# Moving one-operand steps to ScalarE and sharing tile buffers across a layer seam in a four-layer graph kernel

## The chip, the cores and the metric

The kernel runs on one core of one Trainium2 chip. The metric is the device time of one execution in microseconds (us). Engines are named as in the profile: PE is TensorE (PEld its weight loads), DVE is VectorE, ACT is ScalarE, POOL is GpSimd, SP is SyncE, which issues the large loads.

## What is computed

Four graph layers act on `x` (4096 x 64) with one dense 4096 x 4096 matrix `adj`. Each layer normalises `x`, applies relu, and adds its result to `x`. Cut to what matters:

```
h = relu(layernorm(x))
layer 0:  x += relu((adj @ h) @ W0.T + b0)
layer 1:  h', q, k = three "lorentz" linear maps of h
          a = adj * sigmoid(att(q, k));  s = a @ h';  x += s / sqrt(|inner(s, s)|)
layer 2:  log_ij = logmap(h_i, h_j) on the Poincare ball, weights adj / rowsum(adj)
          x += expmap(0, (sum_j w_ij log_ij) @ W2 + b2)
layer 3:  mask = adj != 0;  rank = cumsum(mask) along a row
          weight 0.5 ** (last 100 neighbours, counted from the end);  x += (w @ h) @ W3 + b3
```

All of it is float32, with bfloat16 where values are exact (masks, ranks, split terms).

## The kernel before, in words

**Tiles.** `adj` is read transposed, in groups of 128 partitions x 2 x 512 float32 (512 KB). A block `ib` is 512 columns of the output (8 blocks); a group `g` is 256 rows of the sum (16 groups). A unit of work is one (block, group).

**Layer 0** (`l0_sums`): four matmuls per unit into `acc`; VectorE adds the groups up into `dg` for the degrees. Groups 3, 7, 11, 15 (`LEFT`) of blocks 0 to 6 are added in layer 1 instead (`group`, line 801). At the end of a block `after0` and `before1` turn the rows into layer 1's `HL`, `qT`, `kT`.

**Layer 1**, in pairs of units: `l1_atts` (products `mm<-qT,kT`), `l1_sigmoids` (ScalarE, out of `mm`), `l1_weights` (VectorE, times `adj`), `l1_sums` (`acc<-sig,HL`). Products use two PSUM tiles `mm`, so a product waits until the sigmoid before last has read its tile. There are `SIG` = 6 tiles `sig`. At a block's end `after1` (line 566) copies `acc` to `e`, multiplies by `twice`, copies the result to `h`, squares it, and updates `x`; `before2` (line 450) then makes layer 2's operands `RT`, `LT`, `RB`, `LB`, `HA` and columns `Mc`, `Qc`, `Fc` out of the block's rows. This chain is called the row chain here; nearly all of it is VectorE work on 128 x 256 tiles or on columns of four.

**Layer 2** runs over `work`: 72 items (`ib` <= `J`, two halves). For one item: `l2_dists` (`mm<-RT,LT`, `mm<-RB,LB`), `l2_squares` (ACT Square, `v<-mm`), `l2_clamps` (DVE on `v`), `l2_signs` (PE, adds to the same `mm`), `l2_roots` (ACT Ln, Exp, Exp: `v<-v`, `t<-v`, `v<-v`), `l2_coshs` (DVE `t<-mm,t`), `l2_logs` (ACT `t<-t`), `l2_pairs` (DVE `t<-t,v`), `l2_weights` (DVE `w<-t,adj`), `l2_sums` (PE `acc<-w,HA`). An item with `ib` < `J` is also used turned: `l2_turns` (PE), `l2_weights2` (DVE), `l2_sums2` (PE). Ln and Exp need another table of ScalarE than the sigmoid; `log_exp_tables` loads it. Item 14 is the first that uses the rows of block 7.

The seam: `second_part` (line 956) closes layer 1's pools when the last sum is planned, opens the pool `w2` in the same memory, loads the table and lets VectorE fill `fars`. `v` and `t` (three tiles each) lie in `w2`; `l2_squares` (line 997) therefore asks for `opened["second"]`.

**Layer 3**: `l3_masks` (DVE, `adj` != 0 into the memory of `RT`, `LT`, `RB`, `LB`), `l3_counts` (PE `pick`, DVE copy `total`, PE `spread`, DVE copy `chunks`; twice a block), `l3_ranks` (line 1268: per pair four products with `near`, four with `fars` and `chunks`), `l3_weights` (ACT, two reads of `mm` per pair), `l3_sum` (eight products with `S3`). `l3_ranks` puts one or two sums after each pair of ranks, if their operands are planned.

**Order.** Each engine runs its instructions in a fixed order, which the kernel's own planner makes at build time: `Pace` (line 58) holds when each engine and tile is expected to be free, by rough costs; one load is costed at 1.45 us (line 116). `in_turn` (line 702) takes, of the threads' next steps and of the row chains in `tail`, the one that can start first; a row chain wins ties by `EPS`. So a step whose expected time changes moves to another place in its queue, and steps around it too.

Of the kernel before, what the change touches and what calls it, by code (L numbers as in the profile page):

```python
# [41 lines left out]
MAX_NEIGH = 100  # L42
STEP = 128.0
EPS = 0.01
TURN = "PE"
ON_V, ON_S = "DVE", "ACT"
UP = 2.0 ** (127 - MAX_NEIGH)
# [10 lines left out]
class Pace:  # L58
# [54 lines left out]
        self.latest = max(self.latest, end)  # L113

    def load(self, t):
        self.free["DMA"] = max(self.free["DMA"], self.now) + 1.45
        self.ready[self.name(t)] = self.free["DMA"] + 2.0


# [16 lines left out]
def kernel(ctx: ExitStack, tc: tile.TileContext, a: dict, out: bass.AP):  # L136
# [313 lines left out]
    def before2(ib, st):  # L450
        rb, lb = rbs[slot["now"]], lbs[slot["now"]]
        h = rt("h", [P, CB, D])
        yield from layernorm_relu(ib, h)
        sq = rt("r_sq", [P, CB, D])
        DVE.tensor_mul(sq, h, h)
        n = rt("r_n", [P, CB, 1])
        DVE.tensor_reduce(n, sq, AX.X, ALU.add)
        bc = rt("r_c", [P, CB, 1])
# [14 lines left out]
        DVE.tensor_scalar(m, m, -2.0, None, ALU.mult)  # L473
        yield ON_V
        hh = rt("r2", [P, CB, 2, D])
        for k in range(2):
            DVE.tensor_mul(hh[:, :, k, :], h, ic.to_broadcast([P, CB, D]))
        DVE.tensor_copy(HA[:, cs(ib), 0:D], hh[:, :, 0, :])
        l = rt("l2", [P, CB, D])
        DVE.tensor_scalar(l, hh[:, :, 0, :], -2.0 * SC, None, ALU.mult)  # L480
        yield from transposed(hh.rearrange("p c k d -> p c (k d)"), P, RT[:, ws(ib)])

        v, b = rt("r_v", [P, CB, 2, 1]), rt("r_b", [P, CB, 2, 3])
        DVE.tensor_copy(v[:, :, 0, :], ic)
# [80 lines left out]

    def after1(ib, acc, st):
        e = rows.tile([P, W], F32, tag="e", name="e")
        DVE.tensor_copy(e, acc)
        st["acc_free"][ib % 2] = pace.latest
        yield ON_V, lambda: st["dg_done"].get((1, ib)) if (1, ib) in st["dg"] else 0.0  # L570
        dg = st["dg"].get((1, ib))
        if dg is not None:
            DVE.tensor_add(dg[:, 0, :], dg[:, 0, :], dg[:, 1, :])
        yield TURN
        ps = bank()
        v, n = ps[:, 0 : CB * D].rearrange("p (c k) -> p c k", k=D), CB * D
        for c in range(CB):
            b = slice(c * P, (c + 1) * P)
            PE.matmul(v[:, c, :], e[:, b], twice, start=True, stop=True)
            if dg is not None:  # L580
                PE.matmul(ps[:, n + c : n + c + 1], dg[:, 0, b], ones_f, start=True, stop=True)
        if dg is not None:
            st["dg_free"][ib % 2] = pace.latest
        yield ON_V
        if dg is not None:
            DVE.tensor_add(
                deg[:, cs(ib), :], deg[:, cs(ib), :], ps[:, n : n + CB].unsqueeze(2)
            )
        s = rt("h", [P, CB, D])
        DVE.tensor_copy(s, v)  # L590
        sq = rt("r_sq", [P, CB, D])
        DVE.tensor_mul(sq, s, s)
        n = rt("r_n", [P, CB, 1])
        DVE.tensor_reduce(n, sq[:, :, 1:D], AX.X, ALU.add)
        DVE.tensor_sub(n, n, sq[:, :, 0:1])
        m = rt("r_m", [P, CB, 1])
        DVE.tensor_scalar(m, n, -1.0, None, ALU.mult)
        DVE.tensor_max(n, n, m)
        DVE.tensor_scalar(n, n, 1e-08, None, ALU.max)
        power(n, n, -0.5)  # L600
        yield ON_V
        DVE.tensor_mul(s, s, n.to_broadcast([P, CB, D]))
        DVE.tensor_add(x[:, cs(ib), :], x[:, cs(ib), :], s)
        yield ON_V
# [97 lines left out]
    def in_turn(threads):  # L702

        waiting = [[gen, next(gen, None)] for gen in threads]
        waiting = [t for t in waiting if t[1]]
        while waiting or tail:
            best = None
            for k, entry in enumerate(tail):  # L710
                if k < 2 or entry["evicts"]:
                    need = entry["need"]() if entry["need"] else 0.0
                    if need is None or (entry["on"] == TURN and not spare):
                        continue
                    start = max(entry["at"], pace.free[entry["on"]], need)
                    if best is None or start < best[0]:
                        best = start, entry
            for thread in waiting:
                on, need = thread[1]
                t = need()  # L720
                if t is not None and (best is None or max(t, pace.free[on]) < best[0] - EPS):
                    best = max(t, pace.free[on]), thread
            pace.now, what = best
            if what in tail:
                advance(what)
                continue
            pace.latest = 0.0
            what[1] = next(what[0], None)
            if what[1] is None:
                waiting.remove(what)  # L730
# [54 lines left out]
    def pair_tiles_free():  # L785

        a, b = (d.get("read") for d in pair_tiles[-2:])
        return latest(a, None if b is None else b - 0.8)

    early = ExitStack()  # L790
    p01 = early.enter_context(tc.tile_pool(name="p01", bufs=1))
    w01 = early.enter_context(tc.tile_pool(name="w01", bufs=3))
# [6 lines left out]


    def group(layer, ib, g):
        degree = (g in LEFT and ib < NB - 1) == (layer == 1)
        return {"layer": layer, "ib": ib, "g": g, "degree": degree, "left": 1 + degree, "at": 0.0}


# [94 lines left out]
    def l1_sigmoids():  # L900
        for n, d in enumerate(l1):
            yield "ACT", lambda: latest(
                d.get("dist"), l1[n - SIG].get("summed") if n >= SIG else 0.0
            )
            d["att"] = w01.tile([P, G, W], F32, tag="sig", name="sig", bufs=SIG)
# [10 lines left out]
    def l1_sums():  # L916
        for pair in pairs:
# [5 lines left out]
                d["summed"] = pace.latest  # L923
            if d["last"]:
                ib = d["ib"]
                follow(with_mark(2, ib, after1(ib, acc, st), before2(ib, st)), ON_V, evicts=True)

# [28 lines left out]
    def second_part():  # L956
# [9 lines left out]
        w2["stack"] = ExitStack()  # L966
        w2["pool"] = w2["stack"].enter_context(tc.tile_pool(name="w2", bufs=2))
        w2["others"] = w2["pool"].tile([D + 1, N], F32, name="others", bufs=1)
        log_exp_tables()
        opened["second"] = l1[-1]["summed"]  # L970
        yield "DVE", lambda: 0.0
        DVE.tensor_copy(late["fars"], far.unsqueeze(2).to_broadcast([P, NC, P]))

    def wt(name, **kw):
        return w2["pool"].tile([P, G, W], F32, tag=name, name=name, **kw)

    def l2_dists():
        for d in work:
# [73 lines left out]

    def l2_weights():
        for k, d in enumerate(work):
            yield "DVE", lambda: latest(d.get("paired"), arrival(d), ago(work, k, 2, "summed"))
            d["w"] = wt("w")
            DVE.tensor_mul(d["w"], d["t"], d["adj"])
            d["weighed"] = pace.latest
            used(d)
# [205 lines left out]
            for d in half:  # L1265
                d["chunks"] = chunks

    def l3_ranks():


        for n, pair in enumerate(pairs3):
            yield "PE", lambda: latest(
                ready(pair[0]["chunks"]) if "chunks" in pair[0] else None, pair_tiles_free(),
                work[-1].get("dist"),
            )
            chunks = []
            for d in pair:
                pair_tile(d)
                for c in range(G):
                    chunks.append((d["g"] * G + c, d["ps"][:, c, :]))  # L1280
                    PE.matmul(
                        d["ps"][:, c, :], near, d["m"][:, c, :], start=True,
                        stop=chunks[-1][0] == NC - 1, skip_group_check=True,
                    )
            for q, (c, rank) in enumerate(chunks):
                b = slice(q * Q, (q + 1) * Q)
                if c < NC - 1:
                    PE.matmul(
                        rank, late["fars"][b, c, :], pair[0]["chunks"][b, :], start=False,
                        stop=True, skip_group_check=True,  # L1290
                    )
            for d in pair:
                d["ranked"] = pace.latest
# [33 lines left out]
    def l3_sum():  # L1327
# [25 lines left out]
    last = work[L3_AT:]  # L1353
    order23 = work[:L3_AT] + [d for pair in zip(last, l3) for d in pair] + l3[len(last) :]
    in_turn([
        feed(order, "early"), feed(order23, "second"), second_part(), third_part(), l2_loads2(),
        l0_sums(), l1_sums(), l1_weights(), l1_sigmoids(), l1_atts(),
        in_steps(
            (l2_dists(), -1, once), (l2_signs(), 0, once), (l2_sums2(), 2, if_two(1)),
# [7 lines left out]
        l2_gathers(), l3_weights(), l3_ranks(), l3_counts(), l3_masks(),  # L1367
        degree_sums(0, l0), degree_sums(1, l1), constants(),
    ])

# [44 lines left out]
```

## Time and profile before

| | |
|---|---|
| time, median of 3 runs (lowest, highest) | 1216.04 us (1213.37, 1216.13) |
| profiled execution, its own time | 1215.13 us |
| span of the profiled execution | 1213.4 us |
| mean granted TensorE clock | 0.971 |
| layer 1's last sum ends | 491.15 us |
| first sum of layer 2 starts | 507.53 us |
| HBM read, written | 269.68 MB, 1.05 MB |

The times of single instructions come from the profiled execution, counted from the start of its span. A line of a timeline reads: start, duration, engine, line of the kernel, operation, output<-inputs, shapes, how many were merged, and in brackets the idle time before it with what ended it. A matmul in float32 appears as two records. All operations pass through one helper, so nearly every line says L128, and groups are told apart by their tiles. In a line of groups the numbers after the bar are busy time, mean ns of one, and idle time before with what ended it. In a line by stage the columns are start:end, length, then busy time and count of PE, PEld, DVE, ACT and POOL, the granted clock, the DMA engines' share and GB/s.

### The profile page before, as it was taken

Reading aid. Unit: us, or ns where it says so; the run is one execution under the profiler, and the core shown is the slowest. Engines: PE = TensorE matmul, PEld = TensorE weight load, DVE = VectorE, ACT = ScalarE, POOL = GpSimd, SP = SyncE. Lnnn points to the kernel's source line nnn. Section 1 sums busy time; section 2 is a strip of 40 time slices with the busy share of each in tenths; the row PEclk is TensorE's granted clock in tenths of the full one; section 3 lists DMA queues with packets and bytes.
Section 4 is the critical chain, followed back from the end, with each engine's and each line's share of the span. In section 5 each row is a group of like instructions: output and inputs, shape, how many; then the busy total and the mean of one; then the engine's idle time right before and its main releaser. Section 6 shows DMA issues by size and latency. Waiting matters only on the chain.

```text
span 1213.4 us, 15538 instructions
## 1 busy us (share of the span) xinstructions
PE 1085.3 (89%) x5368; PEld 443.9 (37%) x5368; DVE 980.9 (81%) x1621; ACT 797.6 (66%) x1204; POOL 114.7 (9%) x99
## 2 busy tenths in 40 slices
PE   4799999998999999689989979989888779999998
PEld 1244443333333333234434434444333323333333
DVE  6788789879999998779989999999989984554551
ACT  1055546666656666589898888888877775555554
POOL 2222212101101010000010010000100120000000
PEclk9899999999999999799999999989989899999999
DMA  8899999864767765335534534444444489888830
GB/s 300 326 393 373 366 362 331 328 234 141 266 227 242 250 230 181 122 120 191 178 125 160 197 105 168 145 139 156 140 156 156 144 311 361 305 306 305 300 110 9
DMA packets 77190, 271.75 MB, mean 224 GB/s; under 512 B 10040, under 2 KB 11064, under 8 KB 77112
## 3 DMA queue, kind: packets, MB, share of 16 engines
q1 hardware_dynamic: 75456, 270.57, 62.7%
q8 instruction: 42, 0.69, 0.2%
q10 hardware_dynamic: 1656, 0.20, 0.1%
q14 instruction: 36, 0.29, 0.1%
HBM read 269.68 MB, written 1.05 MB: 223 GB/s over the span
## 4 chain that ended last, share of the span: by engine, by line
PE 48%; DVE 24%; ACT 13%; issue 7%; DMA 5%; POOL 3%; ACTq 0%; SPq 0%; DVEq 0%; POOLq 0%
PE acc L128 25%; PE mm L128 15%; PE tr L128 9%; DMA adj<-in_adjT_dram 4%; DVE w L128 4%; DVE t L128 4%; ACT wt L128 4%; DVE dg L128 3%; DVE sig L128 2%; ACT v L128 2%; ACT sig L128 2%; POOL lo_s L128 2%; ACT t L128 1%; ACT lo_sq L128 1%; DVE v L128 1%
## 5 line engine op out<-in xcount | busy, mean ns | idle before, releaser
L128 PE MATMUL acc<-w,HA 128*65 128x256 f32 (+1 forms) x736 | 258.6, 488 | 20.9 <-DVE w L128 11.7
L128 ACT ACTIVATE sig<-mm,att_b,att_a 128x1024 f32<-128x1024 f32 x128 | 148.4, 1200 | 83.6 <-PE mm L128 74.8
L128 ACT ACTIVATE v<-v 128x1024 f32<-128x1024 f32 x144 | 152.1, 1057 | 47.6 <-DVE v L128 45.0
L128 ACT ACTIVATE wt<-mm 128x1024 uint16<-128x1024 f32 x124 | 120.2, 1021 | 96.1 <-PE mm L128 96.1
L128 DVE TENSOR_TENSOR sig<-sig,adj 128x1024 f32<-128x1024 f32 x128 | 151.9, 1220 | 11.1 <-ACT sig L128 10.8
L128 PE MATMUL acc<-adj,HA 128*64 128x512 f32 x512 | 127.7, 629 | 23.2 <-DVE HA L128 22.4
L128 DVE TENSOR_TENSOR dg<-dg,adj 128x1024 f32<-128x1024 f32 x113 | 137.9, 1221 | 3.4 <-DMA adj<-in_adjT_dram 2.1
L128 PE MATMUL mm<-qT,kT 64*128 64x512 f32 x512 | 131.7, 623 | 8.8 <-ACT sig L128 8.6
L128 PEld LDWEIGHTS acc<-w,HA 128*65 128x65 f32 x736 | 96.8, 142 | 112.2 <-issue 64.6
L128 PE MATMUL acc<-sig,HL 128*64 128x512 f32 x512 | 122.5, 603 | 0.8 <-DVE sig L128 0.8
L128 PE MATMUL acc<-wt,S 128*64 128x512 bf16 x496 | 99.6, 390 | 0.2 <-ACT wt L128 0.2
L128 DVE SCALAR_TENSOR_TENSOR t<-t,v 128x1024 f32<-128x1024 f32 x72 | 89.7, 1246 | 9.8 <-ACT t L128 9.8
L128 DVE SCALAR_TENSOR_TENSOR t<-mm,t 128x1024 f32<-128x1024 f32 x72 | 87.6, 1217 | 4.5 <-PE mm L128 4.2
L128 PE MATMUL mm<-RT,LT 64*128 64x512 f32 x288 | 82.6, 651 | 7.2 <-DVE t L128 7.0
L128 DVE TENSOR_TENSOR w<-t,adj 128x1024 f32<-128x1024 f32 x72 | 87.8, 1220 | 1.4
L128 ACT ACTIVATE t<-t 128x1024 f32<-128x1024 f32 x72 | 75.5, 1049 | 9.4 <-DVE t L128 9.4
L128 DVE TENSOR_TENSOR w<-tr,adj 128x512 f32<-128x512 f32 x112 | 73.2, 684 | 9.9 <-PE tr L128 9.9
L128 DVE TENSOR_SCALAR RT<-adj 128x1024 bf16<-128x1024 f32 x74 | 49.7, 690 | 37.0 <-PE mm L128 36.5
L128 ACT ACTIVATE t<-v 128x1024 f32<-128x1024 f32 x72 | 76.1, 1057 | 2.3
L128 PEld LDWEIGHTS mm<-qT,kT 64*128 64x128 f32 x512 | 42.4, 185 | 86.1 <-ACT sig L128 49.0
L128 ACT ACTIVATE v<-mm 128x1024 f32<-128x1024 f32 x72 | 72.6, 1008 | 1.6 <-PE acc L128 1.6
L128 PE MATMUL tr<-ident,t 128*128 128x128 f32 x448 | 61.0, 279 | 7.7 <-DVE t L128 4.4
(201 smaller groups left out, 1301.3 us busy)
## 6 DMA issues: line engine op xcount, KB each, us to landing
adj<-in_adjT_dram SPq DMA_DIRECT2D x512, 512.0 KB, 4.7
x<-in_x_dram SPq DMA_DIRECT2D x4, 256.0 KB, 4.1
out_dram<-h SPq DMA_DIRECT2D x8, 128.0 KB, 2.9
b<-in_b_dram ACTq DMA_DIRECT2D x2, 32.0 KB, 6.5
W<-in_W_dram ACTq DMA_DIRECT2D x3, 16.0 KB, 4.0
W0T<-in_W0T_dram ACTq DMA_DIRECT2D x2, 16.0 KB, 5.4
W1T<-in_W1T_dram ACTq DMA_DIRECT2D x1, 16.0 KB, 5.2
W1T<-in_b_dram ACTq DMA_DIRECT2D x1, 0.2 KB
```

Source lines behind the costliest of these rows:

```text
L128: done = self.tc.keep_in_program_order(getattr(self.engine, op)(*args, **kw))
```

## The change

1. Row chain: in `after1` the copies `e` and `h` and the square of the result go to ScalarE (the square reads PSUM), and the degree column is copied by ScalarE before VectorE adds it. In `before2` the square of `h`, the second half of `hh`, the copy to `HA` and the scaled copy `l` go to ScalarE; the first half of `hh` stays.
2. `sig`, `v` and `t` come from one pool `pairs` of six tiles that stays open. `v` and `t` of layer 2's first items take the places of the last `sig` tiles, each when that tile's sum is planned. The table load becomes a step of its own, `second_tables`, after the last sigmoid; `l2_weights` is now what asks for `opened["second"]`.
3. The planner costs a load at 1.37; row chains lose ties from the table load until item `FIRST` = 4 is weighed; block 0's degree is summed wholly in layer 0.
4. Layer 3: `l3_ranks` becomes `l3_pass`; where the next ranks are not ready it issues sums.

The diff, cut to its core:

```diff
+FIRST = 4
 ...
-        self.free["DMA"] = max(self.free["DMA"], self.now) + 1.45
+        self.free["DMA"] = max(self.free["DMA"], self.now) + 1.37
 ...
     def before2(ib, st):
-        DVE.tensor_mul(sq, h, h)
+        ACT.activation(sq, h, AF.Square)
+        yield ON_V
 ...
-        for k in range(2):
-            DVE.tensor_mul(hh[:, :, k, :], h, ic.to_broadcast([P, CB, D]))
-        DVE.tensor_copy(HA[:, cs(ib), 0:D], hh[:, :, 0, :])
+        DVE.tensor_mul(hh[:, :, 0, :], h, ic.to_broadcast([P, CB, D]))
+        yield ON_S
+        ACT.copy(hh[:, :, 1, :], hh[:, :, 0, :])
+        ACT.copy(HA[:, cs(ib), 0:D], hh[:, :, 0, :])
-        DVE.tensor_scalar(l, hh[:, :, 0, :], -2.0 * SC, None, ALU.mult)
+        ACT.activation(l, hh[:, :, 0, :], AF.Copy, scale=-2.0 * SC)
 ...
     def after1(ib, acc, st):
-        DVE.tensor_copy(e, acc)
+        ACT.copy(e, acc)
 ...
-            DVE.tensor_add(
-                deg[:, cs(ib), :], deg[:, cs(ib), :], ps[:, n : n + CB].unsqueeze(2)
-            )
-        DVE.tensor_copy(s, v)
-        DVE.tensor_mul(sq, s, s)
+        ACT.copy(s, v)
+        ACT.activation(sq, v, AF.Square)
+            new = rt("r_c", [P, CB, 1])
+            ACT.copy(new, ps[:, n : n + CB].unsqueeze(2))
+            DVE.tensor_add(deg[:, cs(ib), :], deg[:, cs(ib), :], new)
 ...
+                    if "tables" in opened and "weighed" not in work[FIRST]:
+                        start += 2 * EPS
 ...
+    pairp = ctx.enter_context(tc.tile_pool(name="pairs", bufs=SIG))
 ...
-        degree = (g in LEFT and ib < NB - 1) == (layer == 1)
+        degree = (g in LEFT and 0 < ib < NB - 1) == (layer == 1)
 ...
-        log_exp_tables()
+    def second_tables():
+        yield "ACT", lambda: l1[-1].get("read")
+        log_exp_tables()
+        opened["tables"] = pace.free["ACT"]
 ...
     def l2_squares():
-                opened.get("second"), d.get("dist"), ago(work, k, 3, "paired")
+                d.get("dist"), l1[2 * k - SIG].get("summed") if 2 * k < SIG else 0.0,
+                ago(work, k, SIG // 2, "paired"),
-            d["v"] = wt("v", bufs=3)
+            d["v"] = pair_buffer("v")
 ...
     def l2_roots():
-                d.get("clamped"), ago(work, k, 3, "weighed"), ago(work, k, 3, "turned")
+                d.get("clamped"), opened.get("tables"),
+                l1[2 * k + 1 - SIG].get("summed") if 2 * k < SIG else 0.0,
+                ago(work, k, SIG // 2, "weighed"), ago(work, k, SIG // 2, "turned"),
-            d["t"] = wt("t", bufs=3)
+            d["t"] = pair_buffer("t")
 ...
+    def l3_pass():
         for n, pair in enumerate(pairs3):
+            while rank_need(pair) is None:
+                yield "PE", lambda: first_of(rank_need(pair), sum_need() if sums3 else None)
+                if rank_need(pair) is None:
+                    l3_sum()
+            yield "PE", lambda: rank_need(pair)
+            l3_rank(pair)
             for _ in range(1 + n % 2):
-                t = sum_need()
-                if sums3 and t is not None:
+                if sums3 and sum_need() is not None:
                     yield "PE", sum_need
                     l3_sum()
```

More of the change, by code (lines that the diff above doesn't have):

```diff
@@ L475, in before2 @@
         hh = rt("r2", [P, CB, 2, D])
-        for k in range(2):
-            DVE.tensor_mul(hh[:, :, k, :], h, ic.to_broadcast([P, CB, D]))
-        DVE.tensor_copy(HA[:, cs(ib), 0:D], hh[:, :, 0, :])
+        DVE.tensor_mul(hh[:, :, 0, :], h, ic.to_broadcast([P, CB, D]))
+        yield ON_S
+        ACT.copy(hh[:, :, 1, :], hh[:, :, 0, :])
+        ACT.copy(HA[:, cs(ib), 0:D], hh[:, :, 0, :])
         l = rt("l2", [P, CB, D])
-        DVE.tensor_scalar(l, hh[:, :, 0, :], -2.0 * SC, None, ALU.mult)
+        ACT.activation(l, hh[:, :, 0, :], AF.Copy, scale=-2.0 * SC)
         yield from transposed(hh.rearrange("p c k d -> p c (k d)"), P, RT[:, ws(ib)])
+        yield ON_V
         v, b = rt("r_v", [P, CB, 2, 1]), rt("r_b", [P, CB, 2, 3])
@@ L583, in after1 @@
             st["dg_free"][ib % 2] = pace.latest
+        yield ON_S
+        s = rt("h", [P, CB, D])
+        ACT.copy(s, v)
+        sq = rt("r_sq", [P, CB, D])
+        ACT.activation(sq, v, AF.Square)
+        if dg is not None:
+            new = rt("r_c", [P, CB, 1])
+            ACT.copy(new, ps[:, n : n + CB].unsqueeze(2))
         yield ON_V
         if dg is not None:
-            DVE.tensor_add(
-                deg[:, cs(ib), :], deg[:, cs(ib), :], ps[:, n : n + CB].unsqueeze(2)
-            )
-        s = rt("h", [P, CB, D])
-        DVE.tensor_copy(s, v)
-        sq = rt("r_sq", [P, CB, D])
-        DVE.tensor_mul(sq, s, s)
+            DVE.tensor_add(deg[:, cs(ib), :], deg[:, cs(ib), :], new)
         n = rt("r_n", [P, CB, 1])
@@ L788, in pair_tiles_free, with pair_buffer @@
         return latest(a, None if b is None else b - 0.8)
+    pairp = ctx.enter_context(tc.tile_pool(name="pairs", bufs=SIG))
+    def pair_buffer(name):
+        return pairp.tile([P, G, W], F32, tag="pair", name=name)
     early = ExitStack()
@@ L904, in l1_sigmoids @@
             )
-            d["att"] = w01.tile([P, G, W], F32, tag="sig", name="sig", bufs=SIG)
+            d["att"] = pair_buffer("sig")
             ACT.activation(d["att"], d["ps"], AF.Sigmoid, scale=att_a, bias=att_b)
@@ L925, in l1_sums @@
                 ib = d["ib"]
-                follow(with_mark(2, ib, after1(ib, acc, st), before2(ib, st)), ON_V, evicts=True)
+                follow(with_mark(2, ib, after1(ib, acc, st), before2(ib, st)), ON_S, evicts=True)
     half = 0.25 * SC * SC
@@ L972, in second_part @@
         DVE.tensor_copy(late["fars"], far.unsqueeze(2).to_broadcast([P, NC, P]))
-    def wt(name, **kw):
-        return w2["pool"].tile([P, G, W], F32, tag=name, name=name, **kw)
+    def second_tables():
+        yield "ACT", lambda: l1[-1].get("read")
+        log_exp_tables()
+        opened["tables"] = pace.free["ACT"]
     def l2_dists():
@@ L1054, in l2_weights @@
         for k, d in enumerate(work):
-            yield "DVE", lambda: latest(d.get("paired"), arrival(d), ago(work, k, 2, "summed"))
-            d["w"] = wt("w")
+            yield "DVE", lambda: latest(
+                opened.get("second"), d.get("paired"), arrival(d), ago(work, k, 2, "summed")
+            )
+            d["w"] = w2["pool"].tile([P, G, W], F32, tag="w", name="w")
             DVE.tensor_mul(d["w"], d["t"], d["adj"])
@@ L1266, in l3_counts, with rank_need @@
                 d["chunks"] = chunks
-    def l3_ranks():
-        for n, pair in enumerate(pairs3):
[L1272 to L1293, printed above, removed]
+    def rank_need(pair):
+        return latest(
+            ready(pair[0]["chunks"]) if "chunks" in pair[0] else None, pair_tiles_free(),
+            work[-1].get("dist"),
+        )
@@ new lines, in l3_rank @@
+    def l3_rank(pair):
+        chunks = []
+        for d in pair:
+            pair_tile(d)
+            for c in range(G):
+                chunks.append((d["g"] * G + c, d["ps"][:, c, :]))
+                PE.matmul(
+                    d["ps"][:, c, :], near, d["m"][:, c, :], start=True,
+                    stop=chunks[-1][0] == NC - 1, skip_group_check=True,
+                )
+        for q, (c, rank) in enumerate(chunks):
+            b = slice(q * Q, (q + 1) * Q)
+            if c < NC - 1:
+                PE.matmul(
+                    rank, late["fars"][b, c, :], pair[0]["chunks"][b, :], start=False,
+                    stop=True, skip_group_check=True,
+                )
+        for d in pair:
+            d["ranked"] = pace.latest
@@ L1294, in l3_ranks, with first_of @@
+    def first_of(a, b):
+        return b if a is None else a
+    def l3_pass():
+        for n, pair in enumerate(pairs3):
+            while rank_need(pair) is None:
[4 more added lines that the diff above has]
+            l3_rank(pair)
             for _ in range(1 + n % 2):
-                t = sum_need()
-                if sums3 and t is not None:
+                if sums3 and sum_need() is not None:
@@ L1355 @@
     in_turn([
-        feed(order, "early"), feed(order23, "second"), second_part(), third_part(), l2_loads2(),
+        feed(order, "early"), feed(order23, "second"), second_tables(), second_part(), third_part(), l2_loads2(),
         l0_sums(), l1_sums(), l1_weights(), l1_sigmoids(), l1_atts(),
@@ L1366 @@
         ),
-        l2_gathers(), l3_weights(), l3_ranks(), l3_counts(), l3_masks(),
+        l2_gathers(), l3_weights(), l3_pass(), l3_counts(), l3_masks(),
         degree_sums(0, l0), degree_sums(1, l1), constants(),
```

## The prediction

> **What bounds the kernel now.** I read the page's shares and slices first, then busy time by stage, then each queue's timeline around the seams between layers.
>
> ```profile
> PE 1085.3 (89%) x5368; PEld 443.9 (37%) x5368; DVE 980.9 (81%) x1621; ACT 797.6 (66%) x1204; POOL 114.7 (9%) x99
> ...
> PE   4799999998999999689989979989888779999998
> ...
> PEclk9899999999999999799999999989989899999999
> ```
>
> TensorE is the bound at 89%. Its holes are the start, and the dip in the 17th slice (485 to 516 us), where the clock row also falls. Busy time by stage (columns PE, PEld, DVE, ACT, POOL, granted clock):
>
> ```profile
> 280.00:480.00 200.00, 191.01 (x856) 67.61 (x858) 185.15 (x413) 124.71 (x205) 21.01 (x12) 1.00 0.67 226
> ...
> 480.00:500.00 20.00, 13.70 (x68) 5.05 (x64) 13.46 (x21) 11.35 (x26) 1.31 (x1) 0.88 0.61 211
> 500.00:520.00 20.00, 13.39 (x42) 4.46 (x42) 16.63 (x44) 14.96 (x23) 1.01 (x1) 0.69 0.16 52
> ...
> 560.00:600.00 40.00, 40.00 (x193) 19.36 (x192) 36.74 (x42) 36.17 (x39) 0.00 (x0) 1.00 0.52 180
> ```
>
> In layer 1 TensorE is 96% and VectorE 93% busy, ScalarE 62%. In steady layer 2 TensorE has no gap. Between them 12.9 us of 40 are idle and the rest runs at a clock of 0.88 and 0.69. TensorE's timeline shows why:
>
> ```profile
> 489.21 1.94 PE L128 MATMUL acc<-sig,HL 128*64 128x512 f32 x8
> ...
> 500.70 2.08 PE L128 MATMUL mm<-RT,LT 64*128 64x512 f32 x4 [7.01 <-DVE t L128]
> ...
> 507.53 3.68 PE L128 MATMUL acc<-w,HA 128*65 128x512 f32 x4 [4.20 <-DVE w L128]
> ```
>
> Layer 1's last sum ends at 491.15, layer 2's first starts at 507.53. ScalarE and VectorE in that gap:
>
> ```profile
> 485.28 1.19 ACT L128 ACTIVATE sig<-mm,att_b,att_a 128x1024 f32<-128x1024 f32 x1
> ...
> 491.20 1.02 ACT L128 ACTIVATE v<-mm 128x1024 f32<-128x1024 f32 x1 [1.58 <-PE acc L128]
> 496.76 1.06 ACT L128 ACTIVATE v<-v 128x1024 f32<-128x1024 f32 x1 [4.54 <-DVE v L128]
> ...
> 491.81 2.28 DVE L128 COPY fars<-far 128x4096 bf16<-128x4096 bf16 x1
> ```
>
> The square of item 0 (`v<-mm`) has its input early, but its buffer lies where layer 1's tiles lay, so it waits for the last sum. Its clamp then stands behind `fars` and the last row's chain (0.69 + 2.28 + 2.9 us), so Ln starts at 496.76.
>
> Two smaller losses:
>
> ```profile
> 336.71 2.23 PE L128 MATMUL mm<-qT,kT 64*128 64x512 f32 x8 [0.45 <-ACT sig L128]
> ...
> 1123.14 0.38 PE L128 MATMUL tr<-total,spread 128*128 128x512 bf16 x1 [0.80 <-DVE total L128]
> ```
>
> In layer 1 a pair of attention products issued straight after another waits 0.45 and takes 2.23 instead of 1.92: 0.75 us. In layer 3 TensorE waits 0.80 for a total once per block of 28.29 us.
>
> **The seam between layers 1 and 2.** I count from the end of the last sigmoid, 486.47 = 0. Before: layer 2's sum of item 0 starts at 21.1, item 4 (538.28) at 51.8, item 13 at 104.4 (5.85 us an item from item 4). In the changed queues ScalarE has sigmoid, square 0, LB copy, table load, Ln, Exp; VectorE has clamp 0, `fars`, then item 0's work; layer 1's last row enters after about item 3. With the durations above: square 1.0; clamp 0.7, hidden beside LB copy 0.37 and table 1.28, to 2.7; Ln and Exp 2.1, to 4.8. `fars` moves ahead of item 0's chain and waits for the last sum (about 3.4): 5.7. So it is `fars`, not Ln, that is late next. Then cosh 1.22, log 1.05, product 1.22, weights 1.22: sum 0 starts at 10.5. ScalarE then paces items (1.0 + 4 x 1.06 = 5.2 us): 15.7, 20.9; with transposed sums 5.85: item 4 at 32.4, item 13 at 85.0.
>
> The last row is now paid inside layer 2. TensorE has no slack there: 3.3 us (twice, r, l, rb, lb: 1.1 + 0.66 + 0.44 + 0.66 + 0.44). VectorE: about 8.0 less its idle 0.48 an item over nine items, 3.7. ScalarE: 7.8 less 0.56 an item, 2.7. Between 3.3 (all side by side) and 9.7 (none) I take 5.
>
> The clock: after the 7.01 gap four records took 2.08 instead of 1.13. The hand schedule leaves TensorE idle from 3.5 to 6.9, and about 2 more before sum 0. The Trainium skill, "TensorE: Matmul & The Clock Gate", section "Why this matters for your kernels", says that a gap over some 3 us halves the clock. My 3.4 is at that edge. By the rule sum 0 and the products beside it run at half speed (about 4 us, partly behind ScalarE's 5.2); by the row alone, whose gap is twice mine, nothing is certain. I take 2.
>
> Item 13 at 85.0 + 5 + 2 = 92.0 instead of 104.4: **-12.4**. From there to the first counts of layer 3 the order on TensorE, ScalarE and VectorE is the same, so this carries through.
>
> **Row work moved in layer 1.** Eight rows each.
>
> ```profile
> L128 DVE TENSOR_TENSOR r_sq<-h 128x256 f32<-128x256 f32 x16 | 6.8, 425 | 0.5
> L128 ACT ACTIVATE r_sq<-ln_xc 128x256 f32<-128x256 f32 x32 | 13.3, 414 | 58.3 <-DVE ln_xc L128 43.7 <-DMA W<-in_W_dram 6.1 <-DMA W1T<-in_W1T_dram 4.6
> ```
>
> VectorE loses e copy 0.69, h copy 0.42, two squares 0.85, one product 0.42, HA and l 0.57: 2.95 a row, 23.6. ScalarE gains 0.59 + 0.37 + 0.83 + 3 x 0.40 = 3.0 a row, with six small copies of 0.2: 25. The skill, "ScalarE: Activation LUTs", section "Rules for kernel authors", speaks against this: add and multiply belong on VectorE[...]. The rows say equal for squares (414 to 425 ns), so 25 stands. Cover: ScalarE idles 75 of 200 us there; in a 3.8 us pair two sigmoids take 2.3, so up to 1.4 can stand between them, and no moved group exceeds 1.3. Without that cover all 25 would delay sigmoids and the products behind them. The new waits (h copy and r_sq for the `twice` product) hold the sigmoids queued behind; that is this same risk.
>
> In the changed order doubled attention pairs fall from 12 extra to 7: 5 x 0.75 = -3.7. Row 0's degree is summed wholly in layer 0: four matmuls of 0.17 leave layer 1 (-0.7), four adds of 1.22 go to the first 45 us, where VectorE idles (12.6 of 20 busy): taken as nothing, up to +3 if they delay `HA`. **-4.4**.
>
> **Layer 0.** The planner's load pace falls from 1.45 to 1.37. In the order, layer 1's early products no longer fill layer 0: at its last sum one pair of products and three of sums fewer are done, 1.9 + 3 x 1.87 = 7.5 us. They come back only if loads run faster. 86 loads were issued between 60 and 180 us, 1.395 each; the best 20 us had 15, 1.33. 112 loads at 1.35 save 5 at best. So +2.5 to +7.5; I take **+4**, since the DMA share is already 0.98.
>
> **Layer 3.** The loop from one `chunks` product to the next takes 3.0: two ScalarE reads 1.94, near product 0.53, `fars` product 0.40, hand-over. Counts, sums and output work beyond that loop add time. Before, a block's eight intervals are 3.0, 3.14, 3.0, 3.0, 3.0, 4.87, 2.99, 5.29 = 28.3. In the new order counts stand well before the spread, and a sum stands between spread and ranks: 3.5, 3.0, 3.0, 4.57 (0.33 + 1.43 + 0.43 + 1.43 + 0.95), 3.0, 3.0, 3.0, 4.36 = 27.4. About 0.87 for each of seven and a half blocks: **-6.5**. Masks now stand ahead of the chunk copy on VectorE; half idle, it hides them. If not, 0.7 a block comes back.
>
> **Sum.** -12.4 - 4.4 + 4 - 6.5 = -19.3. The profiled execution took 1215.13 (span 1213.4), so 1195.8; that is 0.9 below the runs' median 1216.04. I forecast 1196.
>
> **Rivals.**
> The forecast as summed: chance 0.58, 1190 to 1202.
> (a) The seam gives half: the last row's work collides on all three engines (the full 9.7) and the clock stays low. For it: VectorE and ScalarE are 92% and 90% busy in steady layer 2. Against: three items of lead before row 7's first use as J = 7. 1202; 0.17.
> (b) Half of ScalarE's 25 lands on sigmoids: +12, 1208; 0.09. For it: 14 waits on `sig` already. Against: 1.4 free in each pair.
> (c) Slower: all of the 25 lands uncovered, in-order ScalarE holding each sigmoid behind a row copy that waits for TensorE. 1196 + 25 = 1221. It turns the sign only from 23.7 (1219.7), 95% uncovered. Against: 38% idle ScalarE. 0.04.
> (d) Loads keep up in layer 0 and no clock loss: -4 - 2, about 1189; 0.09.
> (e) The early squares don't start early, since something else gates them (`fars`, or item 0's adjacency): the seam's 12.4 nearly gone, layer 0's cost at its upper end, layer 3's half: about 1214 to 1216, no change; 0.03.
>
> A measurement here tells about 0.3%, 3.6 us, from no change. Faster 0.93, same 0.03, slower 0.04. Range 1187 to 1208.
>
> **What would show it.** Seam: first `v<-mm` before layer 1's last sum, table load at 1 to 3 us after the last sigmoid, first `acc<-w` about 10 after it, a gap under 4 us on TensorE, clock above 0.8. Layer 1: VectorE about 23 lighter, fewer `sig` waits. Layer 0: waits of `acc` for `adj`, 0.7 before, to several us. Layer 3: blocks of 27.4 and no wait for `total`. Wrong if `sig` waits grow, if `fars` holds cosh beyond 7, or if layer 3's period stays 28.3.

## The result and the profile after

The changed kernel takes 1207.7 us (median; 1204.1 to 1212.0) where the kernel before takes 1215.7 in the same session: ratio 0.9932, 95% interval 0.9913 to 0.9950, some 8 us faster. The forecast was 1196 and 19.3 us. One of the changed kernel's eleven executions, the profiled one, was disturbed (2634 us) and is left out here (with it the median is 1208.6), and so every view "of the changed kernel" below is of a second run of the same kernel, `e1_changed_again` (profiled execution 1206.7, span 1205.0, against 1215.1 and 1213.4 before).

The page, the same three lines as before:

```profile
PE 1084.6 (90%) x5360; PEld 445.0 (37%) x5360; DVE 960.1 (80%) x1563; ACT 817.5 (68%) x1266; POOL 112.7 (9%) x99
...
PE   4799999999999999887989989989888779999997
...
PEclk9899999999999999898999989999999889999999
```

Row work has moved as planned: VectorE is 20.8 us lighter, ScalarE 19.9 heavier. The dip in the 17th slice is shallower, and the 19th slice has a new one (9 to 7 in busy share, 9 to 8 in the clock). By stage, the columns as before (busy us of PE, PEld, DVE, ACT, POOL, clock, DMA share, GB/s), first the changed kernel:

```profile
280.00:480.00 200.00, 195.64 (x888) 70.29 (x884) 173.40 (x375) 143.56 (x270) 18.98 (x13) 1.00 0.69 228
480.00:500.00 20.00, 14.84 (x54) 4.00 (x52) 14.50 (x13) 18.48 (x20) 0.00 (x0) 0.83 0.66 220
500.00:520.00 20.00, 18.52 (x94) 8.62 (x91) 18.01 (x24) 17.66 (x21) 1.31 (x1) 1.00 0.41 137
540.00:560.00 20.00, 13.68 (x58) 6.97 (x57) 10.64 (x14) 13.18 (x29) 0.00 (x0) 0.78 0.33 106
```

and one stretch of the kernel before, in which nothing was lost:

```profile
540.00:560.00 20.00, 20.00 (x98) 9.63 (x99) 19.19 (x22) 18.74 (x21) 0.00 (x0) 1.00 0.51 173
```

TensorE's idle time between 480 and 520 fell from 12.9 to 6.6 us, and 6.3 us of idle time at a clock of 0.78 appeared between 540 and 560. That is the story of this change.

The seam's start is close to what the forecast drew. ScalarE of the changed kernel (start, length):

```profile
479.98 1.19 ACT L129 ACTIVATE sig<-mm,att_b,att_a 128x1024 f32<-128x1024 f32 x1
481.94 1.02 ACT L129 ACTIVATE v<-mm 128x1024 f32<-128x1024 f32 x1 [0.77 <-PE mm L129]
...
483.24 1.28 ACT L299 ACT_TABLE_LOAD   x1
484.54 1.06 ACT L129 ACTIVATE v<-v 128x1024 f32<-128x1024 f32 x1
```

VectorE and then TensorE in the same place:

```profile
485.57 2.29 DVE L129 COPY fars<-far 128x4096 bf16<-128x4096 bf16 x1 [1.88 <-PE acc L129]
487.78 1.22 DVE L129 SCALAR_TENSOR_TENSOR t<-mm,t 128x1024 f32<-128x1024 f32 x1
```

```profile
489.14 1.49 PE L129 MATMUL mm<-RT,LT 64*128 64x512 f32 x4 [3.62 <-DVE t L129]
...
492.71 3.65 PE L129 MATMUL acc<-w,HA 128*65 128x512 f32 x4 [1.54 <-issue]
```

Counted from the last sigmoid (481.17), item 0's sum starts at 11.5 (forecast 10.5, before 21.1), after a gap of 3.6 (forecast 3.4). What follows at 555 is new. TensorE, then ScalarE:

```profile
542.62 1.94 PE L129 MATMUL acc<-w,HA 128*65 128x256 f32 x8
...
555.73 3.68 PE L129 MATMUL acc<-w,HA 128*65 128x256 f32 x8 [6.22 <-ACT others L129]
559.20 1.91 PE L129 MATMUL tr<-ident,t 128*128 128x128 f32 x8
```

```profile
548.92 1.04 ACT L129 ACTIVATE t<-t 128x1024 f32<-128x1024 f32 x1
549.87 0.35 ACT L129 CAST LB<-tr 128x256 bf16<-128x256 f32 x1
550.12 1.06 ACT L129 ACTIVATE v<-v 128x1024 f32<-128x1024 f32 x1
...
554.17 1.05 ACT L129 ACTIVATE t<-t 128x1024 f32<-128x1024 f32 x1
555.11 0.57 ACT L129 COPY others<-acc 65x512 f32<-65x512 f32 x1
```

The turned sum that ended at 544.56 has to be copied out of PSUM (`others<-acc`, `l2_gathers`) before the next one may start. ScalarE reaches that copy at 555.11: it stands behind the last row's small copies for `RB` and `LB` and behind a whole item's squares and roots. TensorE waits 6.22 us and comes back at half speed (3.68 for 1.94, 1.91 for 1.04).

### The profile page after: what moved, and what is told of

Read it like the earlier page. It is cut to its first block, busy times and chain, and to the rows that moved or that the text cites. A ratio compares the mean times of both kernels' runs of the same rounds, so it can differ in the third digit from the quotient of the medians.

```text
span 2632.3 us, 15481 instructions
## 1 busy us (share of the span) xinstructions
PE 2586.4 (98%) x5335; PEld 731.5 (28%) x5360; DVE 985.3 (37%) x1563; ACT 839.7 (32%) x1266; POOL 110.7 (4%) x99
## 4 chain that ended last, share of the span: by engine, by line
PE 98%; DVE 1%; issue 1%; ACT 0%; DMA 0%; SPq 0%; DVEq 0%
PE acc L129 55%; PE mm L129 28%; PE tr L129 15%; DMA adj<-in_adjT_dram 0%; ACT v L129 0%; DVE dg L129 0%; DVE t L129 0%; DVE RT L129 0%; DVE e L129 0%; ACT wt L129 0%; ACT t L129 0%; ACT columns L129 0%; SPq L163 0%; DVE LT L129 0%; DVE w L129 0%
## 5 line engine op out<-in xcount | busy, mean ns | idle before, releaser
L129 PE MATMUL acc<-w,HA 128*65 128x256 f32 (+1 forms) x736 | 628.3, 1041 | 6.2 <-ACT others L129 5.9
L129 PE MATMUL acc<-adj,HA 128*64 128x512 f32 x512 | 309.8, 1415 | 13.4 <-DVE HA L129 13.4
L129 PE MATMUL mm<-qT,kT 64*128 64x512 f32 x512 | 315.7, 1398 | 0.0
L129 PE MATMUL acc<-sig,HL 128*64 128x512 f32 x512 | 313.5, 1403 | 0.0
L129 PEld LDWEIGHTS acc<-w,HA 128*65 128x65 f32 x736 | 148.4, 209 | 304.6 <-issue 288.9
L129 PE MATMUL acc<-wt,S 128*128 128x512 bf16 (+1 forms) x480 | 218.6, 767 | 5.3 <-issue 5.3
L129 PE MATMUL mm<-RT,LT 64*128 64x512 f32 x288 | 187.8, 1383 | 3.6 <-DVE t L129 3.6
L129 PE MATMUL tr<-ident,t 128*128 128x128 f32 x448 | 140.7, 538 | 0.8 <-DVE w L129 0.8
L129 PEld LDWEIGHTS tr<-ident,t 128*128 128x128 f32 x448 | 90.9, 210 | 70.4 <-issue 42.5
L129 PE MATMUL mm<-RT,near 128*128 128x512 bf16 x142 | 94.6, 829 | 4.3 <-issue 2.0
```

Of the source, the lines that this page charges most:

```text
L129: done = self.tc.keep_in_program_order(getattr(self.engine, op)(*args, **kw))
```

## The experiments

The table is read from the profiled execution of each run: when the last sigmoid ends; from there to item 13's product with `adj` (`w<-t,adj`, the seam); from there to item 71's (layer 2); from there to the end of VectorE's last step (layer 3; the output's last 2.8 us come on top). Times and ratios come from the timed runs, each against the kernel before in the same session.

| run | median us | ratio (95%) | last sigmoid | seam | layer 2 | layer 3 |
|---|---|---|---|---|---|---|
| before | 1216 | 1 | 486.5 | 101.3 | 386.2 | 236.7 |
| e1_changed_again | 1207.8 | 0.9945 (0.9927–0.9963) | 481.2 | 100.4 | 387.3 | 233.4 |
| e2_layer3_only | 1213.6 | 0.9986 (0.9976–0.9996) | 485.8 | 101.2 | 387.3 | 233.7 |
| e3_seam_only | 1217.1 | 1.0009 (0.9999–1.0018) | 483.7 | 103.3 | 387.6 | 237.2 |
| e4_load_at_1_45 | 1215.9 | 1.0008 (0.9998–1.0018) | 491.1 | 100.3 | 389.0 | 233.4 |
| e5_rows_only | 1208.1 | 0.9941 (0.9928–0.9955) | 484.0 | 96.3 | 386.4 | 237.0 |
| e6_pace_only | 1222.7 | 1.0053 (1.0034–1.0073) | 490.9 | 99.6 | 388.7 | 236.7 |
| e11_rows_and_pace | 1207.2 | 0.9930 (0.9913–0.9948) | 481.9 | 96.3 | 389.7 | 237.4 |
| e13_old_degree_1_45 | 1209.1 | 0.9940 (0.9926–0.9954) | 481.5 | 100.2 | 389.0 | 233.1 |
| e14_old_degree | 1209.0 | 0.9937 (0.9923–0.9951) | 480.6 | 100.4 | 387.3 | 233.4 |
| e9_load_at_1_30 | 1209.4 | 0.9955 (0.9936–0.9974) | 482.1 | 99.9 | 388.9 | 233.1 |
| e7_gather_first | 1204.6 | 0.9902 (0.9881–0.9922) | 485.0 | 96.7 | 388.2 | 233.1 |
| e8_row7_early | 1194.0 | 0.9819 (0.9798–0.9839) | 483.7 | 86.0 | 386.3 | 233.3 |
| e12_row7_out_on_v | 1201.0 | 0.9878 (0.9862–0.9893) | 479.8 | 93.5 | 387.1 | 233.1 |
| e10_roots_split | 1198.2 | 0.9848 (0.9826–0.9870) | 477.7 | 95.7 | 375.3 | 237.5 |
| e15_split_and_out_on_v | 1191.9 | 0.9804 (0.9779–0.9829) | 479.0 | 92.4 | 374.8 | 237.6 |

How far one execution may be trusted: e1, e7, e10, e12 and e15 have the same order of instructions up to the last sigmoid, and it ends at 481.2, 485.0, 477.7, 479.8 and 479.0. So the last-sigmoid column is good to about 4 us; the seam column repeats within 0.5 where the queues are the same (e5 and e11; e1, e13 and e14), layer 3 within 0.8, layer 2 within 3.5.

### First set: where was the gain lost?

The changed kernel once more, unaltered, for a profile.

> The changed kernel unaltered, for an undisturbed profile. It is 0.7% faster, about 8 us, where 19.3 were forecast; this run says which term of the sum failed. Theory A (layer 0 pays more): the seam gives its 12.4, layer 3 its 6.5, and layer 1's first sum region ends 10 us or more later than before, with waits of layer 0's sums on loads of 8 us or more. Theory B (the seam gives half): the first sum of layer 2 starts more than 16 us after the last sigmoid (before 21.1, forecast 10.5), and the granted clock between 480 and 540 stays under 0.8. Theory C (layer 3 gives nothing): its block period stays at 28.3 us.

It answers most of it: -5.3 at the last sigmoid, where the forecast had -0.4; seam -0.9 where it had -12.4; layer 2 +1.1; layer 3 -3.3 where it had -6.5. The sum is -8.4, the difference of the two spans. Theory A (layer 0 pays more) falls. Theory B (the seam gives half) has the place right, and the seam gives still less, but not by the signs it named: item 0's sum starts at 11.5, not after 16, and the clock is 0.83 and 1.00 between 480 and 520. Theory C falls with layer 3's -3.3.

Layer 3's new pass in the kernel before:

```diff
-        l2_gathers(), l3_weights(), l3_ranks(), l3_counts(), l3_masks(),
+        l2_gathers(), l3_weights(), l3_pass(), l3_counts(), l3_masks(),
```

> The kernel before with layer 3's new pass alone. The prediction's step says -6.5 us (0.9947), block period 27.4. Theory C says 0 to -2 us (0.998 to 1.000), period 28 or more. Theories A and B say -6.5.

Layer 3 is 3.0 shorter in the profile. The runs show 1.7 (0.5 to 2.9 by the interval), which is less than the forecast's 6.5 and nearer to theory C; its period of 28 or more is not what the profile shows (27.64). Over all runs its part is 233.1 to 233.7 with the new pass and 236.7 to 237.4 with the old one, the two kernels with split roots apart.

The seam's part alone (pool `pairs`, `second_tables`, the tie rule, `l2_weights` asking for `second`), row chain on VectorE as before:

```diff
-        log_exp_tables()
 ...
+    def second_tables():
+        yield "ACT", lambda: l1[-1].get("read")
+        log_exp_tables()
 ...
-            d["v"] = wt("v", bufs=3)
+            d["v"] = pair_buffer("v")
 ...
```

> The kernel before with the shared six buffers, the table load after the last sigmoid and the tie rule alone; the row chain stays on VectorE, so its last row costs VectorE 2.95 us more inside layer 2. The prediction's step says -12.4 plus up to 3, about -10 us (0.992). Theory B says -4 to -6 us (0.996), with the first sum of layer 2 more than 16 us after the last sigmoid or item 13 later than 98 us after it.

No gain, where the forecast's step said -10 and theory B -4 to -6: item 4's product comes 7.5 us earlier after the last sigmoid (42.3 for 49.8), and item 13's 2.0 later. TensorE waits 4.5 us for `others` here too, though the row work is on VectorE.

The changed kernel with the old pace of loads:

```diff
-        self.free["DMA"] = max(self.free["DMA"], self.now) + 1.37
+        self.free["DMA"] = max(self.free["DMA"], self.now) + 1.45
```

> The changed kernel with the planner's cost of a load put back to 1.45, so that layer 1's early products stand again among layer 0's sums. Theory A says it gains the layer 0 loss back: 6 us or more faster than the changed kernel (1.202 ms or less; ratio to before 0.988 or less). Theories B and C say within 3 us of the changed kernel (0.991 to 0.996).

All 8 us are gone, which no theory had and theory A had the other way round. The last sigmoid comes 9.9 later (491.1), and layer 2 is 1.7 longer, inside its scatter; seam and layer 3 are as in the changed kernel.

### Second set: what eats the seam, what does the pace do?

> The kernel before with one number changed: the planner costs a load at 1.37 us instead of 1.45. My forecast held that the faster pace costs layer 0 about 4 us, since loads could not follow. Theory A now (loads issued earlier do run faster, and layer 0 is bounded by them): layer 0's last sum 4 to 8 us earlier, time 1207 to 1212. Theory B (the pace matters only together with the row work on ScalarE, whose new queue order at 1.45 lost time in layer 0): 1214 to 1217, no change.

Slower by 0.5%, which neither theory had. Layer 0's last sum comes 12 us earlier (205.3 for 217.3), and the last sigmoid 4.4 later: layer 1's first products, which filled layer 0's waits, are all still to do (first sigmoid at 178 instead of 107).

The copy of a turned sum preferred in the planner:

```diff
+LEAD = 1.0
 ...
+                if thread[0] is gathers and on == "ACT":
+                    t -= LEAD
 ...
```

> The changed kernel, with one preference in the planner: the copy of a finished turned sum out of PSUM (others<-acc on ScalarE) is taken 1 us ahead of other steps. Its third one then stands about ten instructions earlier in ScalarE's queue, before the last row's RB and lb steps. Theory A (that late copy is the step that gives the seam back: the 6.22 us wait of the turned sum at 555.73, and the slow matmuls after it, some 2.5 us): 1198 to 1201. Theory B (the last row's own work on three full engines gives it back, whatever its order): the wait turns up elsewhere, 1205 to 1209.

Between the two theories: the wait for `others` is gone, the seam is 3.7 shorter, and the time about 4 us below the changed kernel's, where A said 7 to 10. Of the 9.1 us at that place (6.2 of wait, 2.9 of slow matmuls) 3.7 are gained; the others came back as waits, as B had it. TensorE, then ScalarE of this run:

```profile
543.27 0.66 PE L130 MATMUL tr<-ident,t 128*128 128x128 f32 x4 [2.18 <-ACT RT L130]
```

```profile
541.69 1.06 ACT L130 ACTIVATE v<-v 128x1024 f32<-128x1024 f32 x1
542.65 0.57 ACT L130 COPY RT<-tr 128x512 f32<-128x512 f32 x1
```

Transposes have two tiles `tr` in PSUM, for the items and for the row chain together. The row's transposes for `RT` had ended by 540.7; their copy stands behind an item's three roots until 542.65, and the item's own transpose waits for the tile.

Block 7's preparation taken out of layer 2: its layer-2 operands are made earlier, out of `x` as layer 0 left it, so layer 1's update of block 7 does not enter them:

```diff
 ...
+                if ib == NB - 4:
+                    rows_of.append(with_mark(2, NB - 1, before2(NB - 1, st)))
```

> The changed kernel, with block 7's layer-2 operands made in layer 1 after block 4's row, out of x as layer 0 left it (so block 7's layer-2 operands are not the reference's); of block 7's row chain only the sum's own part (copy, twice, square, update of x) stays in layer 2. It measures what the last row's preparation costs among layer 2's first items. Theory A (late copy): as in the run with that copy preferred, plus about 3 for the row's own matmuls: 1194 to 1199. Theory B (the row's work): the items from 4 to 13 take 5.85 us each again, some 12 us less than in the changed kernel: 1193 to 1197. If neither, the items from 4 to 13 stay slow and the time stays at 1205 to 1209.

This is the size of the disputed term. The time, 1194.0, fits both theories. The seam falls to 86.0, 14.4 less than in the changed kernel, and the items from 4 to 13 take 5.98 us each, as theory B has it. Item 13's sum starts at 87.3, where the forecast without the last row had 85.0, and 2 for the clock. Waits of TensorE in the items concerned, the changed kernel and this one (columns: us, times, longest):

```profile
PE acc L129 <- ACT others L129: 6.2, 1, 6.2
PE acc L129 <- DVE w L129: 1.7, 2, 1.5
PE tr L129 <- ACT RT L129: 1.5, 1, 1.5
PE tr L129 <- DVE w L129: 0.8, 1, 0.8
PE tr L129 <- DVE t L129: 0.2, 1, 0.2
```

```profile
PE tr L129 <- DVE w L129: 0.8, 1, 0.8
```

Items 4 to 13 take 69.3 with the last row among them and 53.8 without: 15.4. Of these, 9.6 are waits (10.4 less 0.8), 2.9 the slow matmuls after the longest wait (1.74 + 0.87 + 0.28), 1.7 the row's own transposes; 1.2 is left over. Each number is from one execution.

> The changed kernel with a load costed at 1.30 us instead of 1.37. The step from 1.45 to 1.37 was worth 8 us in the changed kernel. Theory A (earlier issue lets loads run faster, up to the rate the engines can move): little is left, since the DMA engines' share was already 1.0 from 60 to 180 us at 380 to 410 GB/s: 1204 to 1209. Theory B (the number only reorders layer 0 by chance): anywhere, 1203 to 1216, with layer 0's last sum moved while the rate of loads stays the same.

As the changed kernel (theory A; 1209.4). The step from 1.45 to 1.37 is not continued.

### Third set: rows, and the last row's copies

The row chain on ScalarE in the kernel before, nothing else (the hunks of `before2` and `after1`, without the degree rule):

> The kernel before with the row work on ScalarE and nothing else (loads at 1.45, old seam, old layer 3, old degree rule). My forecast put rows on ScalarE at -4.4 in layer 1. Theory A (rows and pace pay only together, since at 1.45 layer 0 ends as late as before): 1214 to 1217. Theory B (rows pay by themselves, by 4 us): 1210 to 1212.

Beyond theory B: this part alone is worth 7.6 us, as much as the whole change. 4.9 of it are in the old seam, whose VectorE chain of the last row it shortens; I had counted the rows in layer 1 only.

The same with 1.37:

> The kernel before with the row work on ScalarE and a load costed at 1.37, with the old seam, the old layer 3 and the old degree rule. The pace alone made it 0.5% slower. Theory A (together they bring the last sigmoid 5 us forward, and the new seam is worth about 1 and layer 3 about 2 to 3): 1209 to 1212. Theory B (the gain of the changed kernel comes from the seam after all): 1214 to 1218.

No better than the rows alone (0.9930 and 0.9941, and the intervals overlap), and no worse than the whole change. So the new seam adds nothing to the rows: it is 100.4 with them where the old seam is 96.3 with them. These 4.1 us are what layer 3's new pass gains (233.4 for 237.4). Theory A was nearer (1209 to 1212; measured 1207.2), but had the seam's share wrong. The rows and the new pass on the old seam, the kernel that this points to, were not run.

The three roots as three steps of the planner, with the turned sum's copy preferred:

```diff
             ACT.activation(d["v"], d["v"], AF.Ln)
+            yield "ACT", lambda: 0.0
 ...
-        in_steps((l2_logs(), 1, once), (l2_roots(), 0, once), (l2_squares(), -1, once)),
+        in_steps((l2_logs(), 1, once), (l2_roots(), 0, lambda d: 3), (l2_squares(), -1, once)),
```

> The changed kernel with the finished turned sum's copy preferred, as in the run before, and with item's Ln, Exp and Exp on ScalarE as three steps of the planner instead of one, so that a row's copy out of PSUM can stand between them. The two tr banks of PSUM are shared by the items' transposes and the last row's; in the run before TensorE waited 2.2 us for RT, 2.4 for a root and 1.1 for r_sq. Theory A (the banks are held while ScalarE works through a whole item): those waits fall by half, 1201 to 1204. Theory B (the copies stand where they stood, or the engines are simply full): 1204 to 1207.

Better than expected, but elsewhere: the seam gains 0.9 against e7, the rest of layer 2 12.9, and layer 3 gives 4.4 back. Against the changed kernel, TensorE's waits for `v` and `others` between 572 and 945 us fall from 19.7 to 4.3, those for `w` and `t` rise from 5.1 to 25.1, and the mean clock is 0.979 instead of 0.971. So TensorE waits nearly as long, but loses less clock. From item 13 to item 71 its idle time is 42.7 us in the changed kernel and 40.4 here, its busy time 344.6 and 334.9, and the time at half the clock 41.0 and 23.9. Half of the 17.1 us between the last two is 8.5: by this estimate most of layer 2's gain is clock; the last section shows what the clock goes by. The profiled execution is the fastest of five (1190.8; median 1198.2), so the usual gain is smaller than this profile shows.

The last row's four copies out of PSUM on VectorE, with the turned sum's copy preferred:

```diff
+        out_on = ON_V if ib == NB - 1 else ON_S
 ...
```

> The changed kernel with the finished turned sum's copy preferred, and with the last row's copies of RT, LT, RB and LB out of PSUM on VectorE (2.1 us of work) instead of ScalarE. Theory A (what costs is the bank of PSUM held until ScalarE has done an item's three roots): the wait for RT and the one behind the lb transposes go, 1199 to 1203. Theory B (all three engines are full, work is work): VectorE is late instead, 1204 to 1208.

As theory A has it: seam 93.5, 3.2 less than e7, though VectorE is the fuller engine. The copy waits there behind steps of at most 1.2 us, not behind three roots of 3.2. TensorE's two longest waits before transposes fall from 2.4 and 2.2 us to 1.1 and 1.1.

### Fourth set: block 0's degree, and both edits

The changed kernel with block 0's degree left in layer 1 as before, at a load cost of 1.45 (e13) and of 1.37 (e14):

```diff
-        degree = (g in LEFT and 0 < ib < NB - 1) == (layer == 1)
+        degree = (g in LEFT and ib < NB - 1) == (layer == 1)
```

> The changed kernel with a load costed at 1.45 again and with block 0's degree left in layer 1 as before. With the new degree rule and 1.45 the changed kernel took 1215.9, 8 us more than at 1.37, and had 128 of layer 0's matmuls issued at 60 us where the row work alone at 1.45 had 142. Theory A (block 0's degree sums in the start are what layer 0 pays for at 1.45): layer 0's last sum back at 215, time 1207 to 1210. Theory B (the shared buffers or the tie rule lengthen layer 0 at 1.45): 1214 to 1217.

> The changed kernel (load at 1.37) with block 0's degree left in layer 1 as before. Theory A (the faster pace already makes up for the degree sums in the start): same as the changed kernel, 1206 to 1209. Theory B (they still cost layer 0 some 3 us or more): 1202 to 1205.

At 1.45 block 0's degree is what costs e4 its 8 us (layer 0's last sum at 215.5 instead of 221.1); at 1.37 it costs nothing. Neither edit brings anything by itself on top of the rows: the pace pays for the degree.

> The two edits that helped, together: the roots of layer 2 as three steps, and the last row's copies of RT, LT, RB and LB on VectorE. Theory A (they act at different places: VectorE's copies take 2 to 3 us from the last row, the split takes 10 us from the later items of layer 2): 1193 to 1196. Theory B (the split has already freed the banks for the last row): 1197 to 1200.

Below theory A's range, and the fastest kernel of the study: 1191.9, 2% below the kernel before (1.7 to 2.2%) and some 16 us below the changed one.

## Why the prediction was wrong, point by point

**The seam, forecast -12.4, measured -0.9: the step that failed.** Its first half held: item 0's sum at 11.5 for 10.5, item 4's at 35.3 for 32.4, of which the clock is 2.4, forecast apart as 2 (0.36 + 0.21 + 1.72 + 0.14 over the four records after the gap). Its second half did not: item 13's sum came at 103.4 instead of 92.0, and at 104.3 before. The signs that the forecast set for the seam came true (the first sum at 11.5 for "about 10"), but they are of its start; none was set for items 4 to 13. The failing sentence is "The last row is now paid inside layer 2 ... Between 3.3 (all side by side) and 9.7 (none) I take 5." Both ends were sums of busy time. The row costs 15.4, beyond the upper end, and only 1.7 of it is work of TensorE. 9.6 are waits and 2.9 the slow matmuls after the longest: the row holds a `tr` tile or stands in front of the copy that frees `acc`, while ScalarE runs its queue in order. Two edits that only move such copies bring the seam from 100.4 to 96.7 (e7) and 93.5 (e12), 6.9 of the 14.4 that e8 gains without the row; with the split roots it is 8.0 (e15). The other 6.4 were not taken apart. The next sentence, that the rest "carries through", was right from item 13 on (+1.1).

Rival (a) named the place and took the full 9.7 for it; its reason, full engines, is not the whole. e12 speaks against it: work put on the fuller engine made the seam shorter.

**Row work, forecast -4.4 in layer 1.** Alone it is worth 7.6. At the last sigmoid about 2 of it show (484.0 against 485.8 of e2 and 486.5 before, inside the scatter of 4), in the old seam 4.9. In the changed kernel that second part is not to be had again, since the same seam has been rebuilt. ScalarE's 25 us found the cover the forecast gave it: waits on `sig` between 205 and 480 us fell from 8.6 to 3.3, so rivals (b) and (c) fall, though (b)'s 1208 is what was measured: that is luck.

**Layer 0, forecast +4.** With layer 1 the first two layers gained 5.3 in this execution, -1.5 to -8.8 over the five with these queues. Layer 0's last sum ended 6.0 earlier (211.3 for 217.3), where the forecast allowed 5 at best, and its waits for `adj` grew from 0.7 to 2.2 only. "They come back only if loads run faster" was the right question and the DMA share of 0.98 the wrong answer. Before, then changed, 90 to 150 us:

```profile
90.00:120.00 30.00, 28.88 (x158) 13.15 (x156) 26.10 (x45) 17.76 (x69) 6.31 (x5) 1.00 0.97 370
120.00:150.00 30.00, 27.97 (x150) 12.67 (x148) 24.38 (x40) 16.90 (x61) 7.65 (x5) 1.00 0.96 365
```

```profile
90.00:120.00 30.00, 28.22 (x160) 13.65 (x162) 27.43 (x51) 16.39 (x69) 8.38 (x5) 1.00 1.00 387
120.00:150.00 30.00, 27.77 (x154) 12.79 (x152) 26.44 (x39) 12.97 (x48) 8.33 (x5) 1.00 1.02 405
```

At a share of 0.96 to 0.97 there was room for 5 to 11% more bytes, as rival (d) had it for layer 0. That isn't a gain in itself (e6, e14): it lets layer 0 carry block 0's degree, which I had put at 0 to +3 and which is worth 8 at the old pace.

**Layer 3, forecast -6.5, measured -3.3.** The mechanism held and the size was off. One `chunks` copy per block, before and changed:

```profile
1109.69 0.69 DVE L128 CAST chunks<-tr 128x512 bf16<-128x512 f32 x1 [1.59 <-PE tr L128]
...
1137.97 0.69 DVE L128 CAST chunks<-tr 128x512 bf16<-128x512 f32 x1 [1.59 <-PE tr L128]
```

```profile
1101.71 0.69 DVE L129 CAST chunks<-tr 128x512 bf16<-128x512 f32 x1 [1.59 <-PE tr L129]
...
1129.35 0.69 DVE L129 CAST chunks<-tr 128x512 bf16<-128x512 f32 x1 [1.59 <-PE tr L129]
```

The period is 28.28 before and 27.64 after: 0.64 a block, not 0.87. Waits of TensorE from 1000 to 1180 us, before and changed:

```profile
PE tr L128 <- DVE total L128: 6.1, 8, 0.8
PE mm L128 <- ACT wt L128: 2.9, 11, 0.3
```

```profile
PE tr L129 <- DVE RT L129: 2.1, 3, 0.8
PE tr L129 <- DVE LB L129: 0.6, 1, 0.6
PE tr L129 <- DVE LT L129: 0.6, 1, 0.6
PE tr L129 <- DVE RB L129: 0.6, 1, 0.6
```

The waits for `total` are gone, as said. In their place the counts wait for masks (`RT`, `LB`, `LT`, `RB`), 3.9 us over these blocks: "half idle, it hides them" failed. The forecast had named this case ("If not, 0.7 a block comes back"); of its 0.87 the period lost 0.23. And the gain doesn't hold for seven and a half blocks: in the last one the sum between spread and ranks makes the ranks wait 1.17 + 0.32 for ScalarE, and the time from the last `chunks` copy to the end grew from 16.0 to 17.5. 0.64 over seven and a half blocks is 4.8; less 1.5, it is the 3.3 measured.

**The sum.** -0.4, -12.4, -6.5 were forecast for the first two layers, the seam and layer 3; -5.3, -0.9, +1.1 (layer 2) and -3.3 were measured. Errors of 11.5 in the seam, 3.2 in layer 3 and 1.1 in layer 2 were covered in part by 4.9 on the other side. That the time stands near the range's upper end, 1208, is owed to that 4.9.

## What to carry to other kernels

Where a chain of another stage is put among the items of a full pipeline, don't price it by its busy time on each engine: list the buffers it holds (here two PSUM tiles and an accumulator), and for each the instruction that frees it and what stands ahead of that in its queue. Here an engine with short steps freed a shared buffer sooner than an idler engine with long ones (e12). Of parts that were changed together, ask what each would do to the old code: here one small part brought as much as the whole, and a rebuilt seam took away most of what that part had gained in the old one.

## What was not expected of the hardware

The price of a gap on TensorE is not set by its length alone, but also by where it falls. The same wait in layer 2, before and in the changed kernel, with the sum that follows:

```profile
700.70 0.63 PE L128 MATMUL tr<-ident,l 128*64 128x128 f32 x4 [2.00 <-DVE l L128]
701.83 1.93 PE L128 MATMUL acc<-w,HA 128*65 128x512 f32 x4 [0.51 <-DVE w L128]
```

```profile
694.52 1.04 PE L129 MATMUL tr<-ident,l 128*64 128x128 f32 x4 [1.99 <-DVE l L129]
695.66 3.08 PE L129 MATMUL acc<-w,HA 128*65 128x512 f32 x4
```

2.00 us cost nothing in one execution and 1.6 us in the other. The granted clock tells the two apart. In all 16 traces of the table it changes only on a grid with steps of 3.41 us, which lies differently in each execution. In the kernel before, an edge of the grid at 700.16 splits the gap (698.7 to 700.7); in the changed kernel the gap (692.5 to 694.5) lies within one step. The two steps concerned, before and changed (the clock is the third number from the end):

```profile
696.74:700.16 3.42, 1.96 (x10) 0.40 (x8) 3.32 (x9) 2.52 (x4) 0.00 (x0) 1.00 0.20 81
700.16:703.57 3.41, 2.36 (x8) 1.02 (x9) 3.32 (x5) 2.90 (x4) 0.00 (x0) 1.00 0.24 47
```

```profile
691.17:694.58 3.41, 1.42 (x9) 0.36 (x10) 3.27 (x9) 2.86 (x3) 0.00 (x0) 1.00 0.07 29
694.58:697.99 3.41, 3.31 (x7) 1.21 (x8) 2.89 (x4) 2.90 (x5) 0.00 (x0) 0.50 0.33 112
```

Where TensorE was busy for 1.96 us of a step the clock stayed, where it was busy for 1.42 the next step ran at half. Counted over the 16 traces from the first record of the clock on, of the steps at full clock in which TensorE was idle for more than half, 168 of 182 were followed by a step at half the clock, and of the others 59 of 5028. So it is a strong tendency and not an exact threshold. In e7 the seam's gap of 3.62 is split by an edge too: it left the products right after it at full speed (1.13), and the sum that began 3.6 us after its end, behind a second gap of 2.1, took 3.65 instead of 1.93. The Trainium skill ("TensorE: Matmul & The Clock Gate", section "What's actually happening") says that activity is watched in a window that runs freely, which fits; that a gap of 2 us can do it is what these runs add. Gaps like it recur through layer 2, and the clock goes with the time from one execution of a kernel to the next: of 51 executions of the kernel before (the session of e1), the 8 with a mean clock of at most 0.966 took 1217.6 us on average, the 17 with 0.970 or more 1214.3. That the gaps cause this difference was not tried.
